# A decoder layer on one core: a second product buffer, later spread of inverse sums, and transposing transfers on another queue

## The chip, the core and the metric

The kernel runs on one core of a Trainium2 chip. The time is device time in microseconds, the median of the runs; the time before is 1296.32 us (1296.11 to 1297.66, three runs). A profile is one further execution, with every instruction's start and duration.

The engines are named as in the profile: PE (TensorE, the matmuls; PEld is its weight load), DVE (VectorE), ACT (ScalarE), POOL (GpSimd) and SP (SyncE, which here only issues transfers). "SPq" and "ACTq" are the queues of transfers that SP and ACT issue. Each engine works through its own list of instructions in order and waits on semaphores for the others.

## What is computed

The reference is one decoder layer on 16 sequences of 256 rows of 512 numbers: causal attention with 16 heads, then a long convolution with gates over a context, then a feed-forward block whose inputs and weights are rounded to 8-bit steps.

```python
x = x + attention(layernorm(x), q_w, q_b, k_w, k_b, v_w, v_b, o_w, o_b)   # 16 heads of 32, causal softmax
# k = v = context, q = layernorm(x): the 256 rows are 32 heads x 8 channels, l runs over the 512 columns
kv  = einsum('bhil,bhjl->bijhl', k_, v_)              # products of the 8 x 8 channel pairs of a head
out = irfft(rfft(kv) * rfft(ssm_kernel)) + kv * D     # causal convolution along l
x = x + einsum('bijhl,bhil->bjhl', out, q_)
# feed-forward, 1408 wide, with q(v) = round(v / s) * s, s = max|v| / 127 by row
h = silu(q(layernorm(x)) @ q(w_gate)) * (q(layernorm(x)) @ q(w_up))
x = x + q(h) @ q(w_down)
```

In the kernel the FFT is replaced by matmuls with a Toeplitz matrix of the taps. A line number below is that of the kernel before.

## The kernel before

**Order.** The kernel is written with a tile framework. The Python code says in program order what is to be done; a scheduler then simulates the engines, with its own estimate of each instruction's cost, and writes each engine's list of instructions. An instruction that is ready in that simulation can be put ahead of one that stands earlier in the code, and one that lacks a free buffer is put later. On the chip the lists are fixed. Tiles come from pools: a tile with `bufs=n` has n buffers, and a new one has to wait until all readers of the oldest have finished. The memory of a closed pool is given to the next, so tiles of a later pool can wait for those of an earlier one.

**First stage.** Attention goes over 64 units, 16 batches of 4 groups of 4 heads. `plan` says, with lags in units, which step of which unit is written down in each round: `norm_next` (load and normalise a batch), `turn` (cast to a high and a low half in f16, and turn both with transposing transfers, L507), `project` and `values` (three matmuls for each product of split numbers, L473 to L475), `scores` (L568 on PE, mask and minimum L573 on DVE, exponentials with their sums L577 on ACT), `flip` (turn the probabilities on PE, L597 to L605), `weigh` (L618 to L632) and `project_out` (L642, stored by L645). In `scores` the sums of the exponentials, `lsum`, are inverted by DVE (L583) and spread by POOL over the 32 columns of each head into `lb` (L584); `weigh` turns `lb` on PE (L618) and multiplies by it. `lsum` has two buffers, `lb` three.

Woven between are two other jobs. `pairs` makes, for 64 combinations of half, chunk and head, the products of context channels: POOL multiplies into `p` (L688, L692), ACT casts to f16 (`kv[:, :, 0]`, L696), POOL subtracts for the low half (L697), and SP stores it (L698). The operand kT is prepared by `pairs_turn` (L669 on POOL, L673 on PE, L674 on ACT, L675 on POOL). `p` has one buffer:

```python
p = kvp.tile([P, 4, NKV], F32, tag="p", bufs=1, name=f"p{f}_{c}_{h}")
...
nc.scalar.copy(kv[:, :, 0, :], p)
marks["POOL"] = nc.gpsimd.tensor_tensor(kv[:, :, 1, :], p, kv[:, :, 0, :], ALU.subtract).ins
```

The weights of the feed-forward block are rounded, turned with transposing transfers (`weight_flip`, L763) and stored (L767).

**Second stage.** Five units before the end of `plan` the code closes the pools of products and weights and calls `conv_open` and the first `conv_load`. `conv_open` loads `sgt`, a table of 16 numbers for each head parity, to 64 partitions each:

```python
nc.sync.dma_start(
    sgt[64 * j:64 * j + 64, :], bass.AP(sg_d.tensor, sg_d.offset + j, [[0, 64], [2, NK], [1, 1]]))
```

Then 32 tiles of 128 rows follow. For each tile, `conv_load` loads the rows (L178, in the profile bx, with five buffers; rs by L181), squares them on ACT for the norm (L170), scales (L187) and turns on PE (L191); `conv` loads products and taps (L199, L201), multiplies on PE (L219 to L221), gates on DVE (L224 to L230) and adds on POOL (L234 to L241) and DVE (L242); `conv_out` turns the sum and adds the rows (L248, L250). The feed-forward block of the tile follows in steps that lag by up to six tiles: `ffn_x` normalises and rounds (L170, L275, L279, L281) and turns the result by a transposing transfer (xq, L283); `ffn_g` and `ffn_u` are the wide matmuls (L300, L318), with silu on ACT (L304); `ffn_h` rounds (L334, L344) and turns by a transposing transfer (hq, L345); `ffn_d` is the last matmul (L353), with the store (L363). For the last tile, hq is made in four pieces (ehq). All transfers are issued by SP.

Of the kernel before, what the change touches and what calls it, by code (L numbers as in the profile page):

```python
# [8 lines left out]
F32 = mybir.dt.float32  # L9
# [5 lines left out]
ALU = mybir.AluOpType  # L15
# [14 lines left out]
def ap(base, off, dims):  # L30
    return bass.AP(base.tensor, base.offset + off, [list(base.ap[0])] + [list(d) for d in dims])
# [3 lines left out]
def kernel(  # L35
# [4 lines left out]
    nc = tc.nc  # L40
    NB, S, D = x.shape
# [8 lines left out]
    NKV = 288  # L50

    P = 128
# [110 lines left out]

    x1s, x2s, qTs, oTs, rss, kvT = {}, {}, {}, {}, {}, {}
    fst = {}


    def row_norm(src, scratch, nm):
# [98 lines left out]
    def ffn_x(f, k):  # L267
        nm = f"{f}_{k}"
        x2 = x2s[f, k]
        xt = x2[:, :D]  # L270
        xn = ftile([P, D], F32, "xn", 2, nm)
        s = ff.tile([P, 8], F32, tag="s", bufs=DN + 4, name=f"s{nm}")
        st = row_norm(x2, xn, f"f{nm}")
        nc.vector.tensor_scalar(st[:, 3:4], x2[:, D:D + 1], st[:, 2:3], -1.0 / D, ALU.mult, ALU.mult)
        nc.scalar.activation(xn, xt, AF.Identity, bias=st[:, 3:4], scale=st[:, 2:3])  # L275
        nc.vector.tensor_reduce(s[:, 0:1], xn, op=ALU.max, axis=AX.X, apply_absolute_value=True)
        nc.vector.tensor_scalar(s[:, 0:1], s[:, 0:1], 1.0 / QMAX, Q_EPS, ALU.mult, ALU.max)
        nc.vector.reciprocal(s[:, 1:2], s[:, 0:1])
        nc.scalar.activation(xn, xn, AF.Copy, bias=RND, scale=s[:, 1:2])  # L279
        xb = ftile([P, D], BF16, "xb", 2, nm)  # L280
        nc.scalar.activation(xb, xn, AF.Copy, bias=-RND)  # L281
        xq = ftile([P, KC, P], BF16, "xq", U + 2, nm)
        nc.sync.dma_start_transpose(xq, xb)  # L283
        fst[f, k] = dict(nm=nm, xt=xt, s=s, xq=xq)


    def parts(nm):
        n = [slice(a, min(a + 3 * P, I)) for a in range(0, I, 3 * P)]
        return n, n if nm == end else [slice(0, I)]
# [46 lines left out]
    def ffn_h(f, k):  # L336
        st = fst[f, k]
        nm, hp, s = st["nm"], st["hp"], st["s"]
        hb = ftile([P, I], BF16, "hb", 2, nm)
        hq = ftile([P, IC, P], BF16, "hq", 2, nm)  # L340
        for c in parts(nm)[1]:
            if nm == end:
                nc.scalar.activation(hp[:, c], hp[:, c], AF.Copy, bias=RND, scale=s[:, 3:4])
            nc.scalar.activation(hb[:, c], hp[:, c], AF.Copy, bias=-RND)  # L344
            nc.sync.dma_start_transpose(hq[:, c.start // P:c.stop // P, :], hb[:, c])  # L345
        st["hq"] = hq

    def ffn_d(f, k):
# [34 lines left out]
    with ExitStack() as ph:  # L383
# [93 lines left out]
        xts, xhl, vts, lbs, ahl = {}, {}, {}, {}, {}  # L477
        stks, prs, tps = {}, {}, {}
# [19 lines left out]
        def turn(b):  # L498
            xn = xts[b][1]
            xh = ap2.tile([P, 2, D], F16, tag="xh", name=f"xh{b}")  # L500
            xl = ap2.tile([P, 2, D], F16, tag="xl", name=f"xl{b}")
            nc.scalar.copy(xh, xn)
            nc.gpsimd.tensor_tensor(xl, xn, xh, ALU.subtract)
            xhT = ap2.tile([P, 2, KC, P], F16, tag="xhT", name=f"xhT{b}")
            xlT = ap2.tile([P, 2, KC, P], F16, tag="xlT", name=f"xlT{b}")
            for src, dst in ((xh, xhT), (xl, xlT)):
                nc.sync.dma_start_transpose(dst.rearrange("p t c s -> p (t c) s"), src.rearrange("p t d -> p (t d)"))  # L507
            xhl[b] = (xhT, xlT)

        def values(b, t):  # L510
# [41 lines left out]
        def scores(b, g, qc):  # L552
            if qc == 0:
                prs[b, g] = (
                    ap2.tile([P, 4, P], F32, tag="p0", name=f"p0{b}_{g}"),
                    ap2.tile([P, 4, S], F32, tag="p1", name=f"p1{b}_{g}"),
                    ap2.tile([P, 2, 4], F32, tag="nmax", name=f"nmax{b}_{g}"),
                    ap2.tile([P, 2, 4], F32, tag="lsum", name=f"lsum{b}_{g}"))
            stk = stks[b, g]
            nmax, lsum = prs[b, g][2:]  # L560
            nk = P * (qc + 1)
            pr = prs[b, g][qc]
            mk = mask2[:, P - qc * P:2 * P]
            for h2 in range(2):
                ps = ps_s.tile([P, 2, S], F32, tag="s", name=f"s{b}_{g}_{qc}_{h2}")
                for hh in range(2):
                    h = 2 * h2 + hh
                    nc.tensor.matmul(  # L568
                        ps[:, hh, :nk], stk[:, 0, h, qc * P:(qc + 1) * P], stk[:, 1, h, :nk],
                        start=True, stop=True)  # L570
                for hh in range(2):
                    h = 2 * h2 + hh
                    marks["DVE"] = nc.vector.tensor_tensor_reduce(  # L573
                        out=pr[:, h, :], in0=ps[:, hh, :nk], in1=mk, op0=ALU.add, op1=ALU.min,
                        scale=esc[:, 0:1], scalar=BIG, accum_out=nmax[:, qc, h:h + 1]).ins
            for h in range(4):
                marks["ACT"] = nc.scalar.activation(  # L577
                    pr[:, h, :], pr[:, h, :], AF.Exp, scale=-1.0,
                    bias=nmax[:, qc, h:h + 1], accum_out=lsum[:, qc, h:h + 1]).ins
            if qc == 1:  # L580

                lb = ap2.tile([P, 2, P], F32, tag="lb", bufs=3, name=f"lb{b}_{g}")
                nc.vector.reciprocal(lsum, lsum)  # L583
                nc.gpsimd.tensor_scalar(ap(lb, 0, [[P, 2], [32, 4], [1, 32]]), ap(lsum, 0, [[4, 2], [1, 4], [0, 32]]),  # L584
                                        1.0, 1.0, ALU.mult, ALU.mult)
                lbs[b, g] = lb


        def flip(b, g):
            p0, p1 = prs[b, g][:2]  # L590
            t0 = ap2.tile([P, 4, S], F32, tag="t0", name=f"t0{b}_{g}")
            t1 = ap2.tile([P, 4, P], F32, tag="t1", name=f"t1{b}_{g}")
            for h2 in range(2):
                pt = ps_pt.tile([P, 2, S], F32, tag="pt", name=f"pt{b}_{g}_{h2}")
                for hh in range(2):
                    h = 2 * h2 + hh
                    nc.tensor.transpose(pt[:, hh, 0:P], p0[:, h, :], idf)  # L597
                    nc.tensor.transpose(pt[:, hh, P:S], p1[:, h, 0:P], idf)
                if h2 == 0:
                    nc.scalar.copy(t0[:, 2 * h2:2 * h2 + 2, :], pt)  # L600
                else:
                    nc.vector.tensor_copy(t0[:, 2 * h2:2 * h2 + 2, :], pt)
            pt = ps_pt.tile([P, 4, P], F32, tag="pt", name=f"pt{b}_{g}_2")
            for h in range(4):
                nc.tensor.transpose(pt[:, h, :], p1[:, h, P:S], idf)  # L605
            nc.vector.tensor_copy(t1, pt)
            tps[b, g] = t0, t1
# [71 lines left out]
        def pairs(f, c, h):  # L679
                if h == 0:  # L680
                    pairs_load(f, c)
                if h % 2 == 0:
                    pairs_turn(f, c, h // 2)
                kT = kTs[f, c]
                p = kvp.tile([P, 4, NKV], F32, tag="p", bufs=1, name=f"p{f}_{c}_{h}")
                kv = kvp.tile([P, 4, 2, NKV], F16, tag="kv", bufs=2, name=f"kv{f}_{c}_{h}")
                o = (h % 2) * 384
                nc.gpsimd.tensor_tensor(  # L688
                    ap(p, 0, [[NKV, 4], [64, 4], [1, 64]]),
                    ap(kT, o, [[96, 4], [0, 4], [1, 64]]),  # L690
                    ap(kT, o, [[96, 4], [8, 4], [1, 64]]), ALU.mult)
                nc.gpsimd.tensor_tensor(  # L692
                    p[:, :, 256:NKV],
                    ap(kT, o, [[96, 4], [1, 32]]),
                    ap(kT, o + 32, [[96, 4], [1, 32]]), ALU.mult)
                nc.scalar.copy(kv[:, :, 0, :], p)  # L696
                marks["POOL"] = nc.gpsimd.tensor_tensor(kv[:, :, 1, :], p, kv[:, :, 0, :], ALU.subtract).ins  # L697
                marks["SP"] = nc.sync.dma_start(kv_d[f][8 * c + h], kv).ins  # L698
# [61 lines left out]
        def weight_flip(j):  # L760
            q = wst[j]
            qt = ldp.tile([P, IC, P], BF16, tag="qt", name=f"qt_{j}")[:, :q.shape[1] // P, :]
            nc.sync.dma_start_transpose(qt, q)  # L763
            wst[j] = qt

        def weight_out(j):
# [13 lines left out]
        NJ = NG // 2 + D // P  # L780
# [41 lines left out]
        kvp = side.enter_context(tc.tile_pool(name="kvp", bufs=1, side="right", reuse_waits="tile"))  # L822
# [103 lines left out]
```

## Time and profile before

| | |
|---|---|
| median of three runs | 1296.32 us |
| profiled execution: its own time | 1293.03 us |
| its span, and PE's mean granted clock | 1290.9 us, 0.95 of full speed |
| busy in the span: PE, DVE, POOL, ACT | 1127.8, 1044.8, 940.5, 818.5 us |
| last attention matmul, first convolution matmul | 693.6 us, 716.3 us |
| first feed-forward matmul | 753.2 us |
| transposing transfers from SP: attention, weights, second stage | 32, 15, 67 |

Busy time is the sum of an engine's instructions, as a share of the span: 87, 81, 73 and 63%. No share by itself says what limits the time: the two stages have different loads. In the views that follow, "idle before, releaser" names what ended the time for which an engine stood idle, and the landing of a transfer is the time from its issue to the last of its data.

### The profile page before, as it was taken

What the parts mean: (1) busy time and instruction counts of PE and PEld (TensorE: products, weight loads), DVE (VectorE), ACT (ScalarE), POOL (GpSimd) and SP (SyncE); (2) the same over time, 40 slices, a digit from 0 to 9 for tenths busy, and PEclk for the clock granted to TensorE, in tenths of its full rate; (3) what the DMA queues carried; (4) which work ended last, traced back from release to release, by engine and by line L of the source; (5) the groups of instructions that cost most, each with busy time, mean ns of one, the idle gap of its engine ahead of it and who ended that gap; (6) DMA issues with size and microseconds to landing.
All of it is one profiled execution on the core that took longest, in us unless ns stands there. A gap on an engine that the chain in (4) does not pass through costs nothing.

```text
span 1290.9 us, 25306 instructions
## 1 busy us (share of the span) xinstructions
PE 1127.8 (87%) x8487; PEld 775.5 (60%) x8487; DVE 1044.8 (81%) x3034; ACT 818.5 (63%) x1970; POOL 940.5 (73%) x882
## 2 busy tenths in 40 slices
PE   4889789998998989989993688999999899999985
PEld 3656556665666656657661465766666666666652
DVE  5778866876888698788872577999999999999984
ACT  4678766785877778778882444555555545555553
POOL 2367677776886868778772679888788788888862
PEclk8889889999998989989998889999999999999998
DMA  7556767678676876867752956665556555656433
GB/s 237 111 143 201 178 190 212 205 207 214 173 238 183 217 187 201 253 178 206 231 178 73 377 178 161 173 155 158 160 158 176 149 157 153 177 144 161 128 70 74
DMA packets 276904, 229.98 MB, mean 178 GB/s; under 512 B 133069, under 2 KB 231399, under 8 KB 276647
## 3 DMA queue, kind: packets, MB, share of 16 engines
q1 hardware_dynamic: 276775, 228.37, 63.0%
q8 instruction: 67, 1.10, 0.4%
q14 instruction: 62, 0.51, 0.1%
HBM read 124.11 MB, written 75.76 MB: 155 GB/s over the span
## 4 chain that ended last, share of the span: by engine, by line
DVE 36%; PE 23%; DMA 19%; POOL 7%; ACT 6%; issue 5%; SPq 4%; ACTq 0%; DVEq 0%; POOLq 0%
DMA bx<-x_d 6%; DVE u L224 3%; DVE oT L242 3%; DVE g L302 3%; DVE p L573 3%; DMA xt<-in_x_dram 3%; DVE u L227 3%; DMA ct<-in_ctx_dram 2%; PE pj_qk L473 2%; PE pj_qk L474 2%; PE pj_qk L475 2%; DVE hp L321 2%; ACT p L577 2%; DVE s L323 1%; PE s L568 1%
## 5 line engine op out<-in xcount | busy, mean ns | idle before, releaser
L577 ACT ACTIVATE p<-p,nmax 128x128 f32<-128x128 f32 (+1 forms) x512 | 227.9, 449 | 65.5 <-DVE nmax L573 64.4
L697 POOL TENSOR_TENSOR kv<-p,kv 128x1152 f16<-128x1152 f32 x64 | 152.1, 2377 | 91.0 <-ACT kv L696 90.6
L573 DVE CUSTOM_DVE_ANT_0 p<-s,mask,esc 128x128 f32<-128x128 f32 (+1 forms) x512 | 186.8, 410 | 36.5 <-PE s L568 36.0
L219 PE MATMUL c<-bkv,T 128*128 128x288 f16 x640 | 185.4, 290 | 13.3 <-DVE u L230 4.6
L221 PE MATMUL c<-bkv,T 128*128 128x288 f16 x640 | 185.1, 289 | 0.0
L220 PE MATMUL c<-bkv,T 128*128 128x288 f16 x640 | 185.1, 289 | 0.0
L688 POOL TENSOR_TENSOR p<-kT 128x1024 f32<-128x1024 f32 x64 | 144.4, 2257 | 0.9
L238 POOL TENSOR_TENSOR u<-u 128x512 f32<-128x512 f32 x64 | 82.6, 1291 | 46.8 <-DVE u L224 46.6
L568 PE MATMUL s<-st 96*128 96x128 f16 (+1 forms) x512 | 80.4, 254 | 24.6 <-DVE nmax L573 18.0
L305 POOL TENSOR_TENSOR g<-g,sw 128x1408 f32<-128x1408 f32 x30 | 96.2, 3206 | 3.8 <-ACT g L304 3.8
L577 ACT ACTIVATION_READ_ACCUMULATOR p<-p,nmax 128x1 f32 x512 | 98.4, 192 | 0.0
L300 PE MATMUL g<-w,xq 128*128 128x384 bf16 x496 | 89.0, 313 | 9.3 <-DMA xq<-xb 4.2
L318 PE MATMUL u<-w,xq 128*128 128x384 bf16 x496 | 89.3, 316 | 5.4 <-DVE g L302 2.5
L353 PE MATMUL d<-w,hq 128*128 128x512 bf16 x341 | 80.7, 385 | 13.9 <-DMA hq<-hb 9.6
L224 DVE TENSOR_TENSOR u<-c,qT 128x512 f32<-128x512 f32 x128 | 87.2, 681 | 4.9 <-PE c L221 4.6
L219 PEld LDWEIGHTS <-T 128*128 128x128 f16 x640 | 63.3, 99 | 40.3 <-issue 11.0
L170 ACT ACTIVATE bq<-bx 128x512 f32<-128x512 f32 x32 | 23.1, 721 | 96.4 <-DMA bx<-x_d 96.2
L533 ACT ACTIVATE qkhl<-pj_qk,bias 128x256 f16<-128x256 f32 x128 | 59.6, 468 | 33.1 <-DVE qkhl L534 23.1
L473 PE MATMUL pj_qk<-xhT,wq_hi 128*128 128x256 f16 x256 | 71.0, 278 | 8.8 <-DMA xhT<-xh 6.8
L234 POOL TENSOR_TENSOR vsum<-u 128x352 f32<-128x352 f32 x64 | 59.9, 937 | 22.8 <-DVE oT L242 11.5
L568 PEld LDWEIGHTS <-st 96*128 96x128 f16 x512 | 47.8, 101 | 47.7 <-issue 31.1
L474 PE MATMUL pj_qk<-xlT,wq_hi 128*128 128x256 f16 x256 | 71.0, 277 | 5.4 <-DMA xlT<-xl 5.3
(218 smaller groups left out, 3597.7 us busy)
## 6 DMA issues: line engine op xcount, KB each, us to landing
kv_d<-kv SPq DMA_DIRECT2D x64, 576.0 KB, 3.3
bkv<-kv_d SPq DMA_DIRECT2D x64, 576.0 KB, 4.2
qk_d<-qkhl SPq DMA_DIRECT2D x64, 256.0 KB, 2.9
st<-qk_d SPq DMA_DIRECT2D x256, 64.0 KB, 2.5
T<-pad_d SPq DMA_DIRECT2D x64, 256.0 KB, 4.4
x_d<-xt SPq DMA_DIRECT2D x32, 256.5 KB, 2.5
bx<-x_d SPq DMA_DIRECT2D x32, 256.5 KB, 4.3
xt<-in_x_dram SPq DMA_DIRECT2D x16, 512.0 KB, 4.8
```

What stands on the lines that cost most here:

```text
L219: nc.tensor.matmul(reg, T[:, 0, d:d + P], kv[:, mi, 0, :], start=mi == 0, stop=False)
L220: nc.tensor.matmul(reg, T[:, 0, d:d + P], kv[:, mi, 1, :], start=False, stop=False)
L221: nc.tensor.matmul(reg, T[:, 1, d:d + P], kv[:, mi, 0, :], start=False, stop=mi == li)
L224: nc.vector.tensor_tensor(ap(u, uo, [[UW, 2], [64, 4], [1, 64]]), ap(pc, 0, [[512, 2], [64, 4], [1, 64]]), ap(qT, qo, [[96, 2], [8, 4], [1 ...
L305: (nc.gpsimd if (f, k) not in tiles[-ND:] else nc.vector).tensor_tensor(g1[:, c], g1[:, c], sw1[:, I + c.start:I + c.stop], ALU.mult)
L473: nc.tensor.matmul(ps, lh, rh, start=first, stop=False)
L474: nc.tensor.matmul(ps, lh, rl, start=False, stop=False)
L568: nc.tensor.matmul(ps[:, hh, :nk], stk[:, 0, h, qc * P:(qc + 1) * P], stk[:, 1, h, :nk], start=True, stop=True)
L573: marks["DVE"] = nc.vector.tensor_tensor_reduce(out=pr[:, h, :], in0=ps[:, hh, :nk], in1=mk, op0=ALU.add, op1=ALU.min, scale=esc[:, 0:1], ...
L577: marks["ACT"] = nc.scalar.activation(pr[:, h, :], pr[:, h, :], AF.Exp, scale=-1.0, bias=nmax[:, qc, h:h + 1], accum_out=lsum[:, qc, h:h + ...
L688: nc.gpsimd.tensor_tensor(ap(p, 0, [[NKV, 4], [64, 4], [1, 64]]), ap(kT, o, [[96, 4], [0, 4], [1, 64]]), ap(kT, o, [[96, 4], [8, 4], [1, 6 ...
L697: marks["POOL"] = nc.gpsimd.tensor_tensor(kv[:, :, 1, :], p, kv[:, :, 0, :], ALU.subtract).ins
```

## The change

Four edits.

1. `p` in `pairs` gets two buffers.
2. The spreading of `lsum` into `lb` on POOL moves from `scores` to the head of `flip`, and so to a later place in program order. The tile `lb` is still taken in `scores`, after which DVE inverts `lsum`.
3. The transposing transfers of the second stage (xq in `ffn_x`, hq in `ffn_h`, 67 in all) are issued by ACT instead of SP. Those of the first stage stay on SP.
4. The first transposing transfer of ACT in program order gets a dependence on the last ones of SP: the two of the last batch and those of the last two weight tiles, collected in the list `turned`.

The scheduler then writes new lists for all engines, so instructions move that no line of the difference names.

```diff
+    turned = []
 ...
         xq = ftile([P, KC, P], BF16, "xq", U + 2, nm)
-        nc.sync.dma_start_transpose(xq, xb)
+        tr = nc.scalar.dma_start_transpose(xq, xb)
+        for last in turned:
+
+            tc.add_manual_dep(tr.ins, last.ins.name, mybir.DependencyInfo(
+                mybir.DependencyClass.Sync, mybir.DependencyReason.DATA), reason="transposes of two queues")
+        turned.clear()
 ...
-            nc.sync.dma_start_transpose(hq[:, c.start // P:c.stop // P, :], hb[:, c])
+            nc.scalar.dma_start_transpose(hq[:, c.start // P:c.stop // P, :], hb[:, c])
 ...
-                nc.sync.dma_start_transpose(dst.rearrange("p t c s -> p (t c) s"), src.rearrange("p t d -> p (t d)"))
+                tr = nc.sync.dma_start_transpose(dst.rearrange("p t c s -> p (t c) s"), src.rearrange("p t d -> p (t d)"))
+                if b == NB - 1:
+                    turned.append(tr)
 ...
                 lb = ap2.tile([P, 2, P], F32, tag="lb", bufs=3, name=f"lb{b}_{g}")
                 nc.vector.reciprocal(lsum, lsum)
-                nc.gpsimd.tensor_scalar(ap(lb, 0, [[P, 2], [32, 4], [1, 32]]), ap(lsum, 0, [[4, 2], [1, 4], [0, 32]]),
-                                        1.0, 1.0, ALU.mult, ALU.mult)
                 lbs[b, g] = lb
 
 
         def flip(b, g):
-            p0, p1 = prs[b, g][:2]
+            p0, p1, _, lsum = prs[b, g]
+            nc.gpsimd.tensor_scalar(ap(lbs[b, g], 0, [[P, 2], [32, 4], [1, 32]]), ap(lsum, 0, [[4, 2], [1, 4], [0, 32]]),
+                                    1.0, 1.0, ALU.mult, ALU.mult)
 ...
-                p = kvp.tile([P, 4, NKV], F32, tag="p", bufs=1, name=f"p{f}_{c}_{h}")
+                p = kvp.tile([P, 4, NKV], F32, tag="p", bufs=2, name=f"p{f}_{c}_{h}")
 ...
-            nc.sync.dma_start_transpose(qt, q)
+            tr = nc.sync.dma_start_transpose(qt, q)
+            if j >= NJ - 2:
+                turned.append(tr)
```

## The prediction

> **What bounds the kernel now.** I began with the busy time of every engine in stretches, because the kernel has two stages with different limits. The columns are the stretch in us, its length, busy us and instruction count of PE, PEld, DVE, ACT and POOL, then the granted clock, the DMA share and GB/s.
>
> ```profile
> 400.00:600.00 200.00, 186.00 (x1498) 127.20 (x1496) 161.29 (x528) 152.90 (x463) 151.40 (x120) 0.95 0.74 207
> 690.00:710.00 20.00, 3.23 (x28) 1.18 (x25) 1.68 (x4) 0.84 (x2) 0.00 (x0) 0.72 0.10 18
> 710.00:750.00 40.00, 24.24 (x161) 17.93 (x162) 19.70 (x57) 16.01 (x33) 23.78 (x32) 0.80 1.01 351
> 800.00:1200.00 400.00, 372.82 (x2628) 257.12 (x2626) 382.47 (x929) 226.59 (x314) 336.40 (x355) 1.00 0.58 159
> ```
>
> The first stage (attention, to about 694 us) lives on PE, 93% busy. The second (from 716) lives on DVE, 96% busy; ACT has 43% free. Between them is a hole of some 20 us, then 40 us with all sixteen DMA engines full and no compute engine above 61%.
>
> Next the waits, longest first, to see who stops for whom (total us, times, longest):
>
> ```profile
> ACT bq L170 <- DMA bx<-x_d: 96.2, 25, 19.2
> POOL kv L697 <- ACT kv L696: 90.6, 48, 5.6
> POOL lb L584 <- DVE lsum L583: 41.5, 23, 5.7
> ```
>
> POOL stops 132 us behind ACT's cast and DVE's reciprocal, while the next head's products, ready to be made, are held by the single buffer p. So products come out late: the timeline of SP's queue shows their last stores waiting for POOL, and what is queued behind them.
>
> ```profile
> 678.80 7.36 SPq L698 DMA_DIRECT2D kv_d<-kv  x2
> 686.21 0.42 SPq L767 DMA_DIRECT2D w_d<-qt  x1
> 686.68 0.96 SPq L774 DMA_DIRECT2D sw_d<-swt  x1
> 687.68 1.62 SPq L128 DMA_DIRECT2D sgt<-sg_d  x2
> 689.35 3.19 SPq L178 DMA_DIRECT2D bx<-x_d  x1
> 692.58 6.73 SPq L181 DMA_DIRECT2D rs<-rs_d  x1
> ```
>
> The view of tile sgt gives its landing, and PE's timeline the hole that follows:
>
> ```profile
> DMA to landing us min/median/max: 12.7/17.4/22.1
> ```
>
> ```profile
> 693.62 0.59 PE L475 MATMUL pj_o<-wo_hi,al 128*128 128x512 f16 x2
> 715.38 0.90 PE L191 MATMUL sd_q<-idf,bq 128*128 128x128 f32 x3 [21.17 <-ACT bq L187]
> ```
>
> The two sgt loads carry 8 KB, land after up to 22.1 us, and nearly nothing else moves meanwhile (DMA share 0.05 and 0 GB/s from 690 to 706 us, about one engine of sixteen). bx, issued at 689.35, lands at 711.86. Until then ACT waits 19 us at L170.
>
> For the moved transposes, the views of xq and hq have their time on the issuing queue (ns, min/median/max):
>
> ```profile
> L283 SPq DMA_TRANSPOSE xq<-xb x31: 1189/1197/2018, 746.5 to 1244.6; - x31
> L345 SPq DMA_TRANSPOSE hq<-hb x31: 1338/1397/2403, 782.9 to 1275.1; - x31
> ```
>
> **What the Trainium skill says.** "Perfetto Trace Analysis", "Identifying Performance Opportunities": the same bubble repeated can mean too few buffers. The trace agrees: 48 stops at L697. "DMA: Bandwidth & Descriptors", "Issuing engines are not separate DMA queues": another issuer saves only the sequencer's time. So the 3.6 us to landing of xq stay, and only 1.2 to 1.4 us change queue. The same page, "Silent corruption: two transposing streams in flight at once", is why the change adds the waits: the later stream must wait for the other's completion. The same page, "Rules for kernel authors": a strided last dimension becomes one descriptor per element; sgt has 2 x 1024 elements of 4 bytes, which fits its slow landing.
>
> **The change, part by part.** The sum is against the profiled execution, 1293.03 us (span 1290.9), and is then taken from the median 1296.3; the 3.3 us between them I treat as spread.
>
> *Second p buffer, later lb: stage one.* No instruction is added: 64 heads, 64 spreads of 0.415 us. In the built order POOL now mostly makes two products and then does two subtractions, so a cast (1.14 us) lies beside the other head's products (2.73 us) and the 90.6 us of stops largely go; part of the 41.5 goes too. This is no gain while PE is the bound. Following the chain of waits from 60 to 690 us I find 14.6 us in L697, 11.1 in L696, 9.7 in product stores: 35 us is the ceiling. The cost: work bunches. The last subtraction of the products now stands ahead of the last 14 of 64 units' lb, where it stood behind all of them. A head costs POOL 2.26 + 0.47 + 2.38 + 0.56 (L669, L675) = 5.67 us, 363 in all; of 483 us busy to 690 us, 120 are left for other work; 363/50 + 120/64 = 9.1 us per unit against the unit's 10. POOL fits, barely: xl and lb, which PE waits for, can queue behind 2.73 us of products, and exps two units on wait for lb through lsum's two buffers. I bound this at 11 lost (one head's products ahead of xl in four of 16 batches, 4 x 2.73) to 35 gained and take **8 gained**, a quarter of the ceiling, because PE idles only 7 to 13% there.
>
> *The turn of the stages.* Since product buffers are freed earlier, sgt, bx, rs and the first kv and T loads now stand on SP before the last six units' loads. The convolutions of PE follow the last attention matmuls directly, some even before them: the 22 us from 694 to 716 are **gained**. But sgt is as slow there. Directly behind it on SP stand bx, st of a coming unit and the turning of the last batch; on ACT the square of the first bx (L170 before) stands ahead of a values copy and the exps. bx then lands 22 us after sgt's issue; ACT has about 5 us of work ahead of that instruction (copies 0.58 twice, four exps at 0.5, a cast 1.05), and stops some 17 us. PE can run ahead about 4 us more until PSUM is full. So **13 lost**, between 0 (if ACT is late anyway) and 20.
>
> After the turn, 710 to 750 us moved 14 MB at 351 GB/s. Three kv/T pairs (0.83 MB each), five bx (0.26) come earlier, 3.8 MB or 11 us; I take **10 gained**, between 0 and 15.
>
> *Transposes on ACT: stage two.* From 800 to 1200 us 25 tiles pass, 16.0 us each. Per tile ACT is busy 226.6/25 = 9.1 us and gets 1.2 + 1.4 = 2.6 more, and each waits for ACT's own result: 11.9 of 16. The cover is that ACT waits for DVE and bx for 7 us per tile. Queued behind hq's turn are xn (L279), the next silu; behind xq's, the next row's square (L170), which waits 26.9 us per 400 for DVE anyway. On SP the loads are freed of 2.6 us per tile, and of waits for ACT; but bx leaves 0.1 us after the addition that frees its buffer, so SP holds up nothing. **0**, from 10 gained to the rival's loss. The waits for all SP transposes cost nothing: the last of those lands before attention ends, the first on ACT comes after.
>
> *Tail.* The last five turns follow five casts on ACT; hq of the last but one, which SP issued at 1275.08 while ACT went on casting until 1276.4, now comes after them: **1.4 lost**.
>
> Sum: 8 + 22 - 13 + 10 + 0 - 1.4 = 25.6, so **1271 us**.
>
> **Rivals.** *ACT becomes the bound of stage two (slower).* The waits of ACT per tile are 71.4/25 = 2.9 us for bx and 102.8/25 = 4.1 for DVE and PE. 11.9 + 2.9 + 4.1 = 18.9 exceeds 16. If ACT's waits don't shrink as it comes later, up to 2.9 us per tile appear, 90 us over 32; with half of that uncovered, 1271 + 45 = **1316**. It decides from the point where more than 4.1 us of waiting per tile stay. For it: DVE's rn_b waits 13.5 us for ACT's bq already. Against: bx and x2 are released by one addition, so a late ACT waits less for both.
>
> *The hole only moves.* The stall in attention costs the whole 20, stage one gives nothing, loads 5: 22 - 20 + 5 - 1.4 = 5.6, **1291**. For it: the order of ACT and SP; against: PE has matmuls to go on with.
>
> *More than I take.* ACT's stall falls on time lost anyway, and stage one gives 20: 22 + 12 + 20 - 1.4 = 52.6, **1244**. For it: 132 us of POOL stops; against: PE at 93%.
>
> **How the numbers follow.** Forecast 0.55, rival of ACT 0.14, moved hole 0.16, larger gain 0.15. A measurement can tell 0.2% (2.6 us) from no change. Of the moved hole's 0.16, 0.06 lies within that and 0.10 beyond it; all of the forecast and the larger gain is faster. Faster 0.80, same 0.06, slower 0.14. The range 1240 to 1300 holds the forecast, the moved hole and most of the larger gain (0.12); the rival of ACT and 0.03 are left out, 0.17.
>
> **What would show it.** Right: POOL's stops at L697 nearly gone; sgt issued 60 to 80 us before attention's end, a wait of ACT for bx of some 17 us there; no 20 us hole of PE between the stages; stage two still 16 us per tile with ACT near 70%. Wrong: PE under 90% from 200 to 600 us, POOL being waited for by lb or xl; tiles above 16.5 us with DVE waiting for ACT; or a stall of ACT near 0 or above 20 us.

## The result, and the profile after

The changed kernel takes **1314.41 us** (median of 4 runs, 1313.95 to 1317.19) against 1296.26 for the kernel before on the same chip (4 runs): a ratio of 1.0142, 95% interval 1.0124 to 1.016. It is slower by 18 us, where 25 us less were forecast. The profiled execution took 1313.95 us, its span 1312.0. Of all the runs in this document, three of the 16 of f3_after_sgt fell in a slower state (1303 to 1306 us) and are left out of its median.

The new lines carry other numbers: L697 became L705 (the subtraction of the products), L170 became L171, L584 became L597 (the inverse sums), L178 became L179 (the load of bx), L283 and L345 became L284 and L351 (the transposes), L473 to L475 became L479 to L481 (the products of split numbers), and the copy of the values is L526. First the stretches again; the columns are those of the prediction.

```profile
400.00:600.00 200.00, 172.50 (x1419) 119.64 (x1418) 150.28 (x501) 148.54 (x440) 166.81 (x127) 0.96 0.75 222
690.00:710.00 20.00, 19.72 (x174) 13.30 (x172) 13.27 (x50) 16.28 (x53) 0.81 (x2) 1.00 0.27 76
700.00:750.00 50.00, 44.31 (x353) 27.86 (x352) 31.30 (x100) 20.21 (x72) 11.76 (x17) 0.97 0.33 100
750.00:800.00 50.00, 42.34 (x298) 30.98 (x299) 36.47 (x96) 20.18 (x33) 40.32 (x46) 0.90 0.80 259
800.00:1200.00 400.00, 372.35 (x2623) 259.66 (x2621) 371.70 (x929) 223.15 (x312) 338.73 (x362) 0.98 0.62 162
```

From 400 to 600 us PE is busy 172.5 us in place of 186, while POOL has gone from 151 to 167: more product work, less attention. From 690 to 710 there is no hole; attention is still running. The 400 us of stage two are much as before (DVE, their fullest engine, is busy 372 us in place of 382).

The waits, longest first, and one from further down the list:

```profile
ACT bq L171 <- DMA bx<-x_d: 84.6, 27, 21.5
POOL lb L597 <- DVE lsum L591: 64.5, 19, 11.9
...
POOL kv L705 <- ACT kv L704: 44.7, 29, 5.6
...
PE pj_o L479 <- ACT v L526: 19.0, 1, 19.0
```

POOL's stops at the subtraction are halved (90.6 before), but the inverse sums now wait longer for DVE (41.5 before): 109 us of stops in place of 132. The last line is new: PE stands once for 19.0 us, until ACT has copied the values. SP's queue and the view of tile sgt show where that is from.

```profile
642.76 1.41 SPq L128 DMA_DIRECT2D sgt<-sg_d  x2
644.22 3.30 SPq L179 DMA_DIRECT2D bx<-x_d  x1
647.63 14.99 SPq L549 DMA_DIRECT2D st<-qk_d  x5
662.72 2.34 SPq L513 DMA_TRANSPOSE xhT<-xh  x1
```

```profile
DMA to landing us min/median/max: 12.6/16.9/21.3
```

```profile
665.99 0.72 ACT L171 ACTIVATE bq<-bx 128x512 f32<-128x512 f32 x1 [21.48 <-DMA bx<-x_d]
```

sgt is issued 100 us before attention's end (742 us), is as slow as before, and ACT, third fence, stands 21.48 us at the square of the first bx behind it. For stage two, the turning of xq on ACT's queue, from the view of that tile:

```profile
L284 ACTq DMA_TRANSPOSE xq<-xb x31: 1204/1207/3477, 765.8 to 1266.0; - x31
```

The first turn comes 19.3 us later than before (746.5), the last 21.4 later (1244.6). So nearly all of the loss (19.3 of 21.1 us of span) is made before stage two starts. One more view takes it apart: PE's busy time up to attention's last matmul, first of the kernel before, then of the changed one.

```profile
0.00:694.21 694.21, 613.72 (x4935) 424.14 (x4935) 531.96 (x1782) 511.62 (x1540) 483.45 (x395) 0.94 0.70 195
```

```profile
0.00:742.33 742.33, 623.80 (x5012) 433.19 (x5013) 538.78 (x1806) 522.68 (x1563) 489.62 (x405) 0.94 0.67 189
```

Attention ends 48.1 us later. 10.1 of that are PE's work: some of the convolutions' matmuls now stand ahead of attention's last one. 38 are idle time (118.5 against 80.5). From attention's end to the first turn it then takes 23.5 us in place of 52.3, so 28.8 come back: -48.1 + 28.8 = -19.3.

### The profile page after: what moved, and what is told of

It is laid out like the page before. It is cut to its first block, busy times and chain, and to the rows that moved or that the text cites. A ratio compares the mean times of both kernels' runs of the same rounds, so it can differ in the third digit from the quotient of the medians.

```text
span 1312.0 us, 25312 instructions
## 1 busy us (share of the span) xinstructions
PE 1128.5 (86%) x8487; PEld 778.7 (59%) x8487; DVE 1037.7 (79%) x3034; ACT 815.7 (62%) x1970; POOL 940.4 (72%) x882
## 2 busy tenths in 40 slices
DMA packets 276904, 229.98 MB, mean 175 GB/s; under 512 B 133069, under 2 KB 231399, under 8 KB 276647
## 5 line engine op out<-in xcount | busy, mean ns | idle before, releaser
L585 ACT ACTIVATE p<-p,nmax 128x128 f32<-128x128 f32 (+1 forms) x512 | 228.2, 452 | 42.9 <-DVE nmax L581 42.3
L705 POOL TENSOR_TENSOR kv<-p,kv 128x1152 f16<-128x1152 f32 x64 | 152.9, 2394 | 50.1 <-ACT kv L704 44.7
L597 POOL TENSOR_SCALAR lb<-lsum 128x256 f32<-128x256 f32 x64 | 26.4, 413 | 107.7 <-DVE lsum L591 64.5
L324 PE MATMUL u<-w,xq 128*128 128x384 bf16 x496 | 93.1, 318 | 6.5 <-DVE g L308 5.1
L576 PE MATMUL s<-st 96*128 96x128 f16 (+1 forms) x512 | 78.8, 253 | 18.1 <-DVE nmax L581 10.4
L479 PE MATMUL pj_qk<-xhT,wq_hi 128*128 128x256 f16 x256 | 72.0, 282 | 20.3 <-DMA xhT<-xh 10.3
L542 DVE SCALAR_TENSOR_TENSOR qkhl<-pj_qk,bias,qkhl 128x256 f16<-128x256 f32 x128 | 60.5, 473 | 22.3 <-ACT qkhl L541 22.0
L704 ACT CAST kv<-p 128x1152 f16<-128x1152 f32 x64 | 73.4, 1147 | 7.1 <-DMA kv_d<-kv 7.1
```

The source lines that it names most:

```text
L324: nc.tensor.matmul(pg[:, :n].rearrange("p (r o) -> p r o", o=P), xq[:, kc, :], w1[:, (I + c.start) // P:(I + c.stop) // P, kc, :], start=k ...
L585: marks["ACT"] = nc.scalar.activation(pr[:, h, :], pr[:, h, :], AF.Exp, scale=-1.0, bias=nmax[:, qc, h:h + 1], accum_out=lsum[:, qc, h:h + ...
```

## Experiments

The scheduler that writes the engines' lists is called the planner in some expectations. "Idle time" below is always span minus PE's busy time, from the start to attention's last matmul, as in the last two fences. Intervals are of the ratio to the kernel before on the same chip; its median was 1296.9 to 1298.4 us in these sets.

An idle time comes from one profiled execution of each kernel. Up to attention's end, the kernel before, e3, f1 and f2 below run the same lists on all five engines; their idle times are 80.5, 81.3, 84.6 and 87.3 us. So a difference of 7 us or less between two kernels shows nothing by itself.

**Which part of the change costs.** One edit each on the kernel before: `bufs=1` to `bufs=2` for p, and the transposes with their waits on ACT's queue.

> The kernel before with one edit: two buffers for p. If the products' bunching and the earlier sgt load are what costs (theory of the attention stage), it keeps the whole loss: 1310 to 1318 us, attention's last matmul near 740 us, PE's wait for ACT's values copy 19 us. If the transposes on ACT are what costs (rival), it is faster than before: 1271 to 1290 us, attention ending by 700 us.

Measured: 1316.44 us, ratio 1.0137 (1.0118 to 1.0157); attention's end at 746.8 us, idle time 117.1, and one wait of PE for ACT's values copy of 19.15 us.

> The kernel before with one edit: the transposes of stage two on ACT's queue, with their waits. Theory of the attention stage: no difference, 1292 to 1300 us, tiles of 16.0 us as before. Rival (ACT's queue): 1310 to 1320 us, with tiles of 16.5 us and more and DVE waiting longer for ACT.

Measured: 1287.47 us, ratio 0.9916 (0.9886 to 0.9946), faster than either theory said. **The edit of the second buffer alone, with the lists that the scheduler then writes, carries the whole loss; the transposes on ACT gain.** The third part, the spread of the inverse sums in `flip`, was not run: with this edit alone the scheduler writes the lists of before for all five engines, instruction for instruction. The traces agree: e1 leaves the spread in `scores`, and yet runs the same lists as the changed kernel up to the first turn of stage two (765.8 us in the changed kernel).

**What sgt costs.** First the 32 values were stored in another order, so that a partition's 16 lie together:

```
-  bass.AP(sg_d.tensor, sg_d.offset + j, [[0, 64], [2, NK], [1, 1]])
+  bass.AP(sg_d.tensor, sg_d.offset + j * NK, [[0, 64], [1, NK]])
-  nc.sync.dma_start(sg_d, kd[:, 3:4])
+  nc.sync.dma_start(bass.AP(sg_d.tensor, sg_d.offset, [[1, NK], [NK, 2], [1, 1]]), kd[:, 3:4])
```

> The kernel before with the order of sg_d's 32 values in memory changed, so that a partition's 16 values of sgt are one piece of 64 bytes in place of 16 of 4 bytes: 128 pieces in place of 2048. If the count of small pieces makes sgt slow, it lands in 2 to 4 us in place of 12.7 and 22.1, the hole of PE behind attention shrinks from 22 to 3 to 6 us, and the time falls to 1277 to 1281 us. If the latency of a load behind a full queue makes it slow, landing stays above 10 us and the time within 3 us of before.

Measured: sgt landed in 2.6 to 2.7 us and the hole was gone, but the time was 1292.70 us, ratio 0.9944 (0.9922 to 0.9965). Attention ended at 723.8 us with an idle time of 97.8 in place of 80.5: the edited store, at the start of attention, had made the scheduler write other lists for all engines (they part from those of before between 91 and 98 us). Of the 16 us that the quick load is worth (f1 below), 5.7 were left in an order that nobody had asked for.

> The changed kernel with the same edit of sgt. If the stall in attention is the whole of sgt's slow landing, 19 us come back: 1293 to 1298 us, no wait of PE for ACT's values copy, attention's end near 722 us; what is left against the kernel before with the same edit (some 18 us) is the slower pace of attention. If the stall lies on time that is lost anyway, 1305 to 1314 us.

Measured: 1293.74 us, ratio 0.9959 (0.9936 to 0.9981), in the range of the first theory. Its other part did not come: some 18 us were to be left against the kernel before with the same edit, but that kernel, e4, with its redrawn order is at 1292.70.

The load was then made quick without touching the order: every partition gets all 31 or 32 values in one piece, and the reader takes every second one. With this form every engine's list stays as it was.

```
-  sgt = cv.tile([P, NK], F32, bufs=1, name="sgt")
+  sgt = cv.tile([P, 2 * NK], F32, bufs=1, name="sgt")
-  sgt[64 * j:64 * j + 64, :], bass.AP(sg_d.tensor, sg_d.offset + j, [[0, 64], [2, NK], [1, 1]])
+  sgt[64 * j:64 * j + 64, :2 * NK - j], bass.AP(sg_d.tensor, sg_d.offset + j, [[0, 64], [1, 2 * NK - j]])
-  ... rs, sgt[:, k:k + 1], ...
+  ... rs, sgt[:, 2 * k:2 * k + 1], ...
```

> The kernel before with sgt loaded in pieces of 124 to 128 bytes (all 31 or 32 values to every partition, the reader taking every second one), the store of sg_d unchanged: every engine's order stays as before, only the two loads change. If small pieces are the cost: landing of sgt in 2 to 4 us, the hole of PE from 22 to 3 to 6 us, attention's end at 694 us as before, 1276 to 1281 us. If the hole has another cause: within 3 us of before.

Measured: 1280.84 us, ratio 0.9849 (0.9783 to 0.9915). The view of tile sgt of this kernel, and PE's hole behind attention, which was 21.17 us:

```profile
DMA to landing us min/median/max: 3.1/3.3/3.5
```

```profile
704.77 0.72 PE L191 MATMUL sd_q<-idf,bq 128*128 128x128 f32 x4 [3.76 <-ACT bq L187]
```

> The same load of sgt on the kernel before with the transposes on ACT's queue: if the two gains are independent, 1287 less 16 to 19 us, 1267 to 1273 us. If the gain of the transposes needs the hole's time to be there, 1276 to 1281 us as without them.

Measured: 1272.27 us, ratio 0.98 (0.9742 to 0.9857): the two gains add, within their intervals.

> The same load of sgt on the changed kernel, every engine's order unchanged: if the stall in attention costs all of sgt's slow landing, 1293 to 1298 us and PE's wait of 19 us for ACT's values copy gone. If the stall lies on time that is lost anyway: 1305 to 1314 us.

Measured: 1289.27 us, ratio 0.9946 (0.9915 to 0.9978). ACT's longest wait for bx is now, from the list of waits of this kernel:

```profile
ACT bq L171 <- DMA bx<-x_d: 66.5, 28, 4.7
```

The 19 us stop is gone, and 25.1 us of time with it. What stays is attention's pace. The windows up to the last attention matmul, first of f2, whose only differences from f3 are the one buffer and the spread, then of f3:

```profile
0.00:699.99 699.99, 612.70 (x4935) 423.58 (x4935) 530.63 (x1782) 512.80 (x1542) 483.70 (x395) 0.95 0.70 195
```

```profile
0.00:726.11 726.11, 624.18 (x5012) 433.69 (x5013) 538.23 (x1806) 522.94 (x1563) 489.69 (x405) 0.94 0.69 193
```

Idle time 101.9 us: 16.6 of the 38 us were sgt's. The rest is 21.4 us against the kernel before and 14.6 against f2; in time, f3 is 17.0 us above f2. That rest is what the other runs look for; all of them have the quick sgt and the transposes on ACT.

**Is it the density of the products?** With two buffers the scheduler puts all 64 heads into the first 50 units. `tc.issue_after` ties a head's POOL work behind the inverse sum of its unit:

```
+  NH = NU - 6
-  for f, c, h in share(heads, u, NS):
-      pairs(f, c, h)
+  for f, c, h in share(heads, u, NH):      # while u < NH
+      with tc.issue_after(lbi[units[u]]):
+          pairs(f, c, h)
```

> The run before this one, with the heads of the products shared over 58 units in place of 54 and each head's work on POOL queued behind the inverse sum of its own unit: two buffers stay, but POOL makes 1.1 heads per unit in place of 1.3. If the bunching of the products is what slows attention: PE above 90% from 200 to 600 us again, attention's last matmul near 700 us, 1270 to 1280 us. If two buffers slow attention in another way, or any other order than that of before does: PE at 86 to 88%, 1290 to 1300 us.

Measured: 1286.77 us, ratio 0.9925 (0.9901 to 0.9948); idle time 101.0. The time lies between the two ranges, 2.5 us below f3 (the intervals overlap), and the idle time is f3's.

> One buffer for p, transposes on ACT, the quick load of sgt, and POOL's products tied to their own units as in the paced run with two buffers. It is a redrawn order with a single buffer. If two buffers by themselves slow attention: PE's idle time up to attention's last matmul stays near the 87 us of the same kernel without the ties, 1270 to 1277 us. If the order of the kernel before is a good one and most others cost PE some 15 to 20 us: idle time 97 to 105 us, 1280 to 1292 us.

Measured: 1269.10 us, ratio 0.9781 (0.9731 to 0.9831); idle time 89.4. A new order with one buffer can be as good as the old one. (PE is below 90% from 200 to 600 us here too, 173.3 and 177.0 of 200 each; it makes up for it before 200 us.)

**Is it one of the waits that grew?** PE's waits up to 640 us, where the changed kernel with the quick sgt loses nearly all of the rest; first the list of this kernel, f3_after_sgt, then the line that answers to its first one in the kernel before:

```profile
PE pj_qk L480 <- DMA xlT<-xl: 16.5, 7, 4.1
PE pj_qk L479 <- DMA xhT<-xh: 10.3, 4, 5.7
...
PE s L576 <- DVE nmax L581: 7.8, 9, 2.5
PE pt L606 <- ACT p L585: 7.6, 6, 4.1
PE pj_qk L479 <- DVE qkhl L542: 7.5, 4, 3.4
```

```profile
PE pj_qk L474 <- DMA xlT<-xl: 5.3, 4, 3.5
```

This wait grew by 11 us. xl is made on POOL behind products and turned on SP behind the products' stores, so both were taken out of its way: the stores issued by ACT (`nc.scalar.dma_start(kv_d[f][8 * c + h], kv)`), and xl made by DVE (`nc.vector.tensor_tensor(xl, xn, xh, ALU.subtract)`).

> Two buffers, transposes on ACT, the quick load of sgt, and the stores of the products issued by ACT in place of SP, so that on SP the transposition of xl no longer stands behind a store that waits for POOL. If that queue is part of what slows attention: from xl's subtraction to the issue of its turn 2 us in place of 4.9, PE's waits for xlT from 16.5 to some 8 us, time 1281 to 1287 us. If the order decides: other waits in their place, PE's idle time still 97 to 105 us, 1287 to 1298 us. ACT's own list gets waits for POOL in it, which could cost as much.

Measured: 1315.46 us, ratio 1.0142 (1.0099 to 1.0185). xlT's waits fell to 8.0 us, as expected, but the idle time rose to 113.5, and the time is above both ranges. The stores now stand in ACT's list and all lists were redrawn, so this run does not say what the stores on SP cost.

> Two buffers, transposes on ACT, the quick load of sgt, and xl's subtraction on DVE in place of POOL, so that it can't stand behind products. If xl behind products is what slows attention: PE's waits for xlT from 16.5 to under 6 us, idle time to attention's end from 102 to about 88, time 1276 to 1283 us. If the order decides: idle time 97 to 105 us, with waits for DVE in place of those for xlT, 1288 to 1298 us.

Measured: 1302.61 us, ratio 1.0035 (1.0014 to 1.0056), above both ranges; idle time 104.0. The same list of this kernel:

```profile
PE s L576 <- DVE nmax L581: 18.8, 19, 5.4
PE pj_v L479 <- DVE qkhl L542: 10.4, 6, 3.4
...
PE s L576 <- DMA st<-qk_d: 7.7, 6, 2.2
```

xlT is out of the head of the list (3.9 us from 60 to 640 us), and waits for DVE stand in its place. But the edit also gives DVE more work (561.9 us busy up to attention's end, 538.2 in f3), so g3 alone can't tell what xl on POOL costs. For that it needs the same edit with one buffer.

> The same edit with a single buffer for p. If xl behind products matters only with two buffers: within 5 us of the 1272 of the same kernel without the edit, idle time near 87 us. If the order of the kernel before is a good one among worse: idle time 97 to 105 us, 1280 to 1292 us.

Measured: 1296.30 us, ratio 1.0 (0.998 to 1.0021); idle time 103.0. So with one buffer the edit costs 24.0 us of time and 15.7 of idle time by itself (against f2). With xl on DVE, the second buffer then adds 6.3 us of time and 1.0 of idle time (g3 against g4); with xl on POOL it added 17.0 and 14.6 (f3 against f2). This is what one would see if xl behind the products were a part of the cause. As each of these edits redraws the lists, it is not shown; but it is not ruled out either.

**Buffers and density apart.** Ties as above, heads over 63 units or pressed into 50 (there the inverse sums are also tied behind the products, with `tc.issue_after(marks["POOL"])`, so that the products can't slip back). In h1 and h4, `conv_open` and the closing of the pools also move from five units before the end to one.

> Two buffers, heads of the products spread evenly over 63 of 64 units by ties on POOL (1.0 per unit), the convolutions' loads behind them; transposes on ACT and quick sgt as before in this series. If the density of products is what slows attention: PE's idle time to attention's last matmul 80 to 91 us and 1265 to 1277 us. If two buffers do it whatever the density: idle time 98 to 105 us, 1280 to 1292 us.

> One buffer, the 64 heads pressed into the first 50 units by ties on POOL in both directions (1.28 per unit, the density that the changed kernel has), the rest as in the run before. If density is the cause: idle time 98 to 110 us, attention's end at 722 us or later, 1285 to 1305 us. If it is the second buffer: idle time 80 to 91 us, and with the earlier loads of the convolutions 1258 to 1272 us.

> Two buffers, the 64 heads pressed into 50 units in the same way. Both theories: idle time 98 to 110 us, 1285 to 1300 us, like the changed kernel with the quick sgt (1293); if it is far from that, the ties themselves matter and the set can't be read.

> One buffer, heads spread evenly over 63 units by the same ties, the convolutions' loads behind them. Both theories: idle time 80 to 91 us, 1265 to 1277 us, like the tied run with one buffer and 58 units (1269); if it is far from that, the ties themselves matter.

Measured (heads per unit as built):

| run | buffers | heads per unit | idle us | us | ratio (95%) |
|---|---|---|---|---|---|
| h1_p2_even | 2 | 1.0 | 96.1 | 1297.26 | 0.9994 (0.9975 to 1.0012) |
| h3_p2_dense | 2 | 1.28 | 94.4 | 1298.17 | 0.9996 (0.9975 to 1.0017) |
| h4_p1_even | 1 | 1.0 | 90.5 | 1303.05 | 1.0033 (1.0014 to 1.0053) |
| h2_p1_dense | 1 | 1.28 | 137.4 | 1363.58 | 1.0496 (1.0466 to 1.0525) |

Of these eight numbers only two lie in a range named beforehand (h3's time, h4's idle time): the ties themselves matter. With two buffers, density makes no difference to PE's idle time (96.1 and 94.4), so bunched products are not the one cause, as I had thought. With one buffer, dense products forced by these ties cost far more (137.4). The total times of h1 and h4 say less about attention, because the convolutions' first loads moved behind the last product stores: in h4 they stand behind the feed-forward weights as well, sgt lands 12.2 us after its issue even in large pieces, and PE has this hole in its timeline:

```profile
732.59 1.11 PE L192 MATMUL sd_q<-idf,bq 128*128 128x128 f32 x4 [26.61 <-ACT bq L188]
```

**Is it products made ahead?** Two buffers, but each product tied behind the subtraction before it.

```
+  with tc.issue_after(marks["POOL"]):
       nc.gpsimd.tensor_tensor(ap(p, 0, ...), ap(kT, ...), ap(kT, ...), ALU.mult)
```

> The kernel of f2_act_sgt (transposes on ACT, quick sgt) with a second buffer for p, and each head's product queued behind the subtraction of the head before it, so that POOL alternates product and subtraction as with one buffer and never makes two products in a row. If products made ahead are what costs: idle time of PE 80 to 91 us, 1262 to 1276 us. If a second buffer costs through the order that the planner then draws: idle time 94 to 105 us, 1283 to 1297 us.

Measured: 1305.49 us, ratio 1.0057 (1.0036 to 1.0077); idle time 113.3, both above what either theory named, while the stops of POOL at the subtraction were back (89.6 us). From the list of waits up to 640 us of this kernel:

```profile
PE s L576 <- DVE nmax L581: 21.7, 18, 5.5
PE pj_qk L480 <- DMA xlT<-xl: 12.9, 9, 3.5
PE pt L605 <- DVE t L610: 12.2, 7, 6.3
```

> The kernel of g1_p1_paced (1269 us) with a second buffer and the same alternation. Expected of products made ahead: 1262 to 1276 us, idle time near 89 us. Expected of the planner's order: idle time 94 to 105 us, 1283 to 1297 us.

Measured: 1292.71 us, ratio 0.9947 (0.9921 to 0.9972), 23.6 us more than the same kernel with one buffer, g1; idle time 104.2. Both are in the ranges of the second theory. Products made ahead are not the one cause either.

**What stands.** Five different orders with one buffer (the old one, g1, h4, e4, g4; not the forced h2) have idle times of 80 to 87 (the old one, in four kernels), 89.4, 90.5, 97.8 and 103.0 us. Nine with two buffers have 94 to 114, the changed kernel's own 102 without sgt's stop. By idle time the old order is the best of all that were tried, and no order with two buffers reached it. But the two groups overlap, and 94.4 (h3) and 90.5 (h4) differ by less than kernels with the same lists do. Nor has the second buffer a fixed price. In five pairs of kernels it is the only difference apart from the lists that follow from it (f2 and f3 also differ in the spread, which changed no list in the test above):

| one buffer, two buffers | us | idle us |
|---|---|---|
| f2, f3 | +17.0 | +14.6 |
| g1, f4 | +17.7 | +11.6 |
| g4, g3 | +6.3 | +1.0 |
| h4, h1 | -5.8 | +5.7 |
| h2, h3 | -65.4 | -43.1 |

So what the second buffer costs depends on the order that comes with it. The old lists with two buffers were not run, and what in the new order costs PE its time is open. Density (h1, h3) and products made ahead (i1, i2) are ruled out as the one cause. The stores on SP and xl on POOL are not: the runs that took them away brought costs of their own.

## Why the prediction was wrong

**Stage one, the step that failed ("second p buffer, later lb"): 8 gained was forecast, 15 to 21 were lost.** (The loss is f3's idle time, 101.9, less f2's 87.3 or before's 80.5.) The premise that POOL's stops go was half right: 132 us became 109. But the ceiling of 35 us was taken from the chain of waits, and a quarter of it booked as gain, although PE, at 93%, hardly stops for the products: from 60 to 690 us its list of waits in the kernel before names them once, with 0.4 us. The risk was priced as xl behind a product in four of 16 batches, 11 us. PE's waits for xlT did grow by about that (5.3 to 17.0 us), so this part of the risk was foreseen, and then outweighed by the gain. Waits for the exps (1.6 to 9.4 us in all) and for the turned probabilities that DVE copies (2.3 to 8.5) grew as well, while those for DVE's minimum fell (18.0 to 10.4). What I put at nothing: the edit lets the scheduler write new lists for all engines, and the old list was, by idle time, the best of those measured. e4 shows the size of this term with no change in buffers at all: 10 to 17 us of idle time (97.8 against 80.5 to 87.3) from a store of 128 bytes. The bound of 11 us on the lost side was too narrow; which part of the new order costs PE the rest stays open. The Trainium skill ("Perfetto Trace Analysis", "Identifying Performance Opportunities") takes a repeated gap on the engine that should be saturated as a hint of too few buffers. Here the gap was real, 48 stops, and the buffer cut it to 29, but it lay on POOL and not on PE, the fullest engine of this stage, and the time rose.

**The stop at sgt: 13 forecast, 17 to 25 measured** (16.6 us of idle time, 25.1 us of time between the changed kernel and f3). The mechanism was right to the instruction: sgt, then bx, then st and the turn of the last batch on SP; the square, then the values copy on ACT. Mis-sized was ACT's work ahead of the square: I put 5 us after sgt's issue, and ACT was there after 1.8 (sgt was issued at 642.76; ACT's wait of 21.48 ends at 665.99, and so began at 644.51). PE ran on for 4 us, as forecast.

**The hole and the loads: 22 + 10 forecast, 18.7 measured** (28.8 us less from attention's end to the first turn, of which 10.1 had only moved into attention). The hole did go. The 10 us of loads did not come: from 700 to 750 us the DMA engines moved 100 GB/s, and 259 after 750. The feed-forward weights are issued from 744 us on, behind attention's last stores, and the next bx at 758.5, after the first tile has had its rows added (756.4 us) and so freed one of the five bx buffers, which had been full since 675. That these late loads are what kept the 10 us away was not tested.

**Transposes on ACT: 0 forecast, a gain of 9 to 11 us measured with the old order** (before to e3 10.9, with an interval clear of no change; f1 to f2 8.6, with intervals that overlap). In the changed kernel it is not to be seen: e1 and the changed kernel have ratios of 1.0137 and 1.0142. ACT did not become the bound; its 223 us per 400 are as before. The rival that said so named 1316 us, and the result is 1314: a right number with a wrong mechanism, which e1 and e3 part cleanly. The profile of f2 has first to last turn in 494.7 us against 501.3 in f1. The tail, where 1.4 us were to be lost, is part of the gain: from the last turn to the end it takes 42.6 and 42.3 us in e3 and f2, and 46.3 and 46.8 in before and f1 (46.0 in the changed kernel). Whether the gain is SP's freed 2.6 us per tile or the new lists of stage two was not tried.

**The rivals.** "The hole only moves" took all 20 us for sgt's stop, which is about right, and stage one at zero; it missed by stage one's loss as well. The range ended at 1300: apart from ACT's rival no case came to more, and stage one could lose 11 us at most. For the two traces, the sum with measured terms is -21.4 - 16.6 + 18.7 - 1.8 (from the first turn to the end, 544.4 us before and 546.2 after) = -21.1, the difference of the two spans.

Two of the signs of being wrong came: PE under 90% from 200 to 600 us, and a stall of ACT above 20 us (21.48). The first is a weak sign, for g1, the fastest kernel here, shows it too.

A version that beats both kernels came out on the way: before, plus the transposes on ACT, plus the quick sgt, is f2 at 1272.27 us; with the products tied to their units it is g1 at 1269.10, not to be told apart from f2 by their intervals.

## What to carry to other kernels

A stop on an engine that the bounding engine doesn't wait for is not a reserve, however often it repeats; price a buffer by whose wait it ends. To see what a new order costs, look at several orders: a single pair of kernels can give either sign. Where a scheduler writes the lists, an edit's first effect is a new order, so measure each part alone, and prefer edits that leave the lists as they are (the second form of sgt) to those that redraw them (the first). When load after load lands late, look at the small one ahead of them in the queue first.

## What the runs showed of the hardware

- 8 KB in 2048 pieces of 4 bytes took 12.5 to 22.1 us to land (four kernels). 16 KB in 128 pieces of 124 to 128 bytes took 2.3 to 4.0 us in 13 of the 14 kernels that load sgt so, and 12.2 in h4, where it stands behind the feed-forward weights. The Trainium skill ("DMA: Bandwidth & Descriptors", "Rules for kernel authors") says that a strided last dimension becomes one descriptor per element; the runs agree: f1 moves 274984 DMA packets where before moves 276904, a difference of 1920 and so of 2048 less 128. The 16.4 us that f1 gains are the price here. What the runs add is that the next load pays too: the first bx landed 21.5 to 22.5 us after its issue behind the small pieces, and 3.5 to 4.3 behind the large ones (10.8 in h4).
- The same lists do not give the same end of attention: in before, e3, f2 and f1 it came at 694.2, 698.0, 700.0 and 701.0 us. PE's busy time for the 4935 matmuls up to it lay between 612.7 and 616.7 us, the shortest at a granted clock of 0.95 and the longest at 0.93; the rest is idle time. A few us of attention's end belong to no edit.
